# Pairwise bilinear products: later tiles of x loaded one by one from a second queue, with regular output slots

## The chip, the cores and the metric

The kernel runs on one core of a Trainium2 chip. The metric is the time of one execution on the device in microseconds (us), the median of several runs. A core has five engines that run their own instruction streams: TensorE (PE; its weight loads are PEld), VectorE (DVE), ScalarE (ACT), GpSimd (POOL) and SyncE (SP). Sixteen DMA engines move data between the chip's large memory (HBM) and the core's on-chip memory. A DMA transfer is started by an instruction on one engine's queue, and goes on beside everything else.

## The reference

For 4096 samples of 32 fields with 64 features each, every field is multiplied by a 64 x 64 matrix, and each of the 496 pairs of fields (i < j) gives one product by elements:

```python
vid = jnp.einsum('bfd,de->bfe', x, W)
idx_i, idx_j = jnp.triu_indices(F_, k=1)
return x[:, idx_i, :] * vid[:, idx_j, :]
```

Everything is float32. The input x has 33.6 MB, the output 520 MB.

## The kernel before

**Layout.** The host lays x out so that the 128 partitions are 2 halves of the batch x 64 features. A tile is 128 samples of each half; there are 16 tiles. One field of one tile is a *unit*: 128 float32 (512 B) in each partition. A tile of x has 32 units, 16,384 B per partition; its output has 496 units, one for each pair.

**On-chip memory.** One tensor, `mem`, holds 445 units for everything. Places for tiles of x and *slots* for output are cut out of it by hand: `XPLACE` says where each tile of x stands, and `SLOTS` lists for each output transfer its size in pairs and its place in `mem`. Places overlap in the course of time: an instruction that writes to a part of `mem` waits for the transfer that still reads that part, and for no other.

**Work on a tile.** TensorE multiplies the tile by W in 16 matmuls (L162) into `vid`, which has one place only[...]. VectorE then writes the products x[i] * vid[j] (L186) into the current slot, many pairs in one instruction, in the order that `by_block()` and `products()` give. When a slot is full, SyncE starts the transfer of it to the output (L189). An output transfer is cut in rows, one per partition: a slot of 127 pairs has rows of 127 x 512 = 65,024 B.

**Loads.** All transfers stand on SyncE's queue, in the order of the program. Tile 0 comes in two halves (L138). Then `GROUPS` says which tiles are loaded together: the first group, tiles 1 to 5, is loaded at the start. The second (tiles 6 to 10, in two transfers) is started at L192 to L194 when tile 4 is done, and the third (tiles 11 to 15, in two transfers) when tile 9 is done. A group is thus five tiles back to back. `SLOTS` has 80 entries whose sizes, 51 to 127 pairs, are chosen so that places for five tiles come free together before a group is loaded.

Of the kernel before, what the change touches and what calls it, by code (L numbers as in the profile page):

```python
# [16 lines left out]
UNITS = 445  # L17


GROUPS = [  # L20
    [[0], [1, 2], [3, 4], [5]],
    [[6, 7], [8, 9, 10]],
    [[12, 11], [15, 14, 13]],
]
XPLACE = [285, 317, 349, 381, 413, 0, 285, 317, 349, 381, 413, 128, 96, 64, 32, 0]


SLOTS = [
    (127, 32), (126, 159), (63, 32), (64, 95), (84, 159), (63, 32),
    (74, 243), (84, 159), (95, 32), (71, 243), (116, 127), (95, 32),  # L30
    (106, 243), (116, 127), (95, 32), (106, 243), (116, 127), (95, 32),
    (127, 243), (116, 127), (95, 32), (127, 243), (116, 127), (43, 370),
    (95, 32), (95, 127), (63, 222), (95, 32), (84, 127), (74, 211),
    (84, 32), (95, 116), (74, 211), (116, 0), (95, 116), (74, 211),
    (116, 0), (95, 116), (105, 211), (105, 0), (105, 105), (105, 211),
    (105, 0), (105, 105), (127, 211), (105, 0), (105, 105), (127, 211),
    (105, 0), (106, 105), (56, 211), (95, 267), (51, 362), (107, 160),
    (73, 267), (73, 340), (84, 160), (84, 244), (95, 340), (84, 160),
    (95, 244), (105, 340), (84, 160), (96, 244), (105, 340), (105, 128),
    (106, 233), (105, 339), (127, 96), (116, 223), (106, 339), (127, 96),  # L40
    (116, 223), (106, 339), (127, 64), (127, 191), (127, 318), (127, 32),
    (127, 159), (120, 286),
]


PAD = 24
# [2 lines left out]

STARTS = [0, *accumulate(n for n, _ in SLOTS)]  # L50


def by_block():


    def within(lo):
        yield "step", lo, 2, 1, 0
        for k in range(2):
            yield "step", lo, 4, 2, k
        for i in (lo, lo + 8):  # L60
            yield "row", i + 4, i, 4, 4
        yield "row", lo + 8, lo, 8, 8

    yield from within(0)
    yield "row", 16, 0, 16, 16
    yield from within(16)


def products(blocks, at=0):

    for kind, a, b, c, d in blocks:
        if kind == "row":
            rows, n, i0, di, j0, dj = c, d, b, 0, a, 1
        else:
            rows, n, i0, di, j0, dj = 16 // b, c, a, b, a + c + d, b
        r = k = 0
        while r < rows:
            room = STARTS[bisect_right(STARTS, at)] - at
            if k or room < n:
                m, w = 1, min(n - k, room)  # L80
            else:
                m, w = min(rows - r, room // n), n
            yield at, m, w, i0 + r * di + k, di, j0 + r * dj, dj
            at += m * w
            if k + w == n:
                r, k = r + m, 0
            else:
                k += w
# [10 lines left out]
@with_exitstack  # L99
def pairwise_bilinear_kernel(  # L100
    ctx: ExitStack,
    tc: tile.TileContext,
    x0: bass.AP,
    x: bass.AP,
    w: bass.AP,
    out: bass.AP,
):

    nc = tc.nc
    NT = sum(len(tiles) for group in GROUPS for tiles in group)
    F = x0.shape[1] - PAD0
    D = P // 2
    NP = F * (F - 1) // 2

    BANK = 512 // C


    ctx.enter_context(tc.manual_schedule(engines={mybir.EngineType.SP}))

    const = ctx.enter_context(tc.tile_pool(name="const", bufs=1))
    psum = ctx.enter_context(
        tc.tile_pool(name="ps", bufs=1, space=bass.MemoryType.PSUM)
    )
    vid = psum.tile([P, F, C], F32)

    mem = const.tile([P, UNITS, C], F32)  # L130


    w2 = const.tile([P, D], F32)


    for lo in (0, F // 2):
        place = XPLACE[0] + lo
        nc.sync.dma_start(out=mem[:, place : place + F // 2, :], in_=x0[:, lo : lo + F // 2, :])  # L138
        if lo == 0:
            nc.sync.dma_start(out=w2, in_=w)  # L140
    loaded = 1

    def load(tiles):
        nonlocal loaded
        n = len(tiles) * F
        place = XPLACE[tiles[0]]
        at = (loaded - 1) * F
        nc.sync.dma_start(out=mem[:, place : place + n, :], in_=x[:, at : at + n, :])
        loaded += len(tiles)

    groups = iter(GROUPS)
    for tiles in next(groups)[1:]:
        load(tiles)

    for t in range(NT):
        xt = mem[:, XPLACE[t] : XPLACE[t] + F, :]


        for b in range(0, F, BANK):
            for h in range(2):  # L160
                half = slice(h * D, (h + 1) * D)
                nc.tensor.matmul(  # L162
                    vid[half, b : b + BANK, :],
                    lhsT=w2[half, :],
                    rhs=xt[half, b : b + BANK, :],
                    start=True,
                    stop=True,
                )

        for at, m, w, i, di, j, dj in products(by_block(), t * NP):  # L170
            slot = bisect_right(STARTS, at) - 1
            n = m * w
            begin, end = STARTS[slot], STARTS[slot + 1]
            ot = mem[:, SLOTS[slot][1] : SLOTS[slot][1] + SLOTS[slot][0], :]
            o = ot[:, at - begin : at - begin + n, :]
            if m == 1:
                left = xt[:, i : i + w, :]
                right = vid[:, j : j + 1, :].to_broadcast([P, w, C])
            else:
                o = o.rearrange("p (m w) c -> p m w c", m=m)  # L180
                right = vid[:, j : j + (m - 1) * dj + 1 : dj, :].unsqueeze(2).to_broadcast([P, m, w, C])
                if di == 0:
                    left = xt[:, i : i + w, :].unsqueeze(1).to_broadcast([P, m, w, C])
                else:
                    left = xt.rearrange("p (m d) c -> p m d c", d=di)[:, i // di : i // di + m, i % di : i % di + w, :]
            nc.vector.tensor_tensor(o, left, right, ALU.mult)  # L186
            at += n
            if at == end:
                nc.sync.dma_start(out=out[:, begin:end, :], in_=ot)  # L189


        if t + 2 == loaded < NT:  # L192
            for tiles in next(groups):
                load(tiles)  # L194


_INS = ["r_x", "L0_rec_W"]
# [42 lines left out]
```

## Time and profile before

| | |
|---|---|
| Time, median of 3 runs | 1288.43 us (1288.34 to 1288.59) |
| Span in the profile | 1287.0 us |
| DMA, over the span | 553.79 MB, mean 430 GB/s |
| HBM | 33.59 MB read, 520.09 MB written |
| VectorE busy | 1087.8 us (85%), 407 instructions |
| TensorE busy | 225.4 us (18%), 512 matmuls |
| Output transfers | 80, of 3264 to 8128 KB |
| Loads of x after tile 0 | 7: 2048 KB x1, 4096 KB x4, 6144 KB x2 |

A group in the profile is a line, an engine, an operation and its tensors, with the number of instructions; then busy time and the mean duration of one; then the idle time of the engine just before these instructions, with what ended most of it. The slices give the busy share of each of 40 equal parts of the span in tenths (9 is 90% or more), and for DMA the rate too. q1 is the hardware queue of SyncE; q8 and q14 carry the chip's own fetching of instructions.

### The profile page before, as it was taken

The numbers are of one execution on the slowest core, as the hardware profiler recorded it, in microseconds if no ns is written. First come the engines' busy times: TensorE is split into PE (matmuls) and PEld (weight loads), VectorE is DVE, ScalarE is ACT, GpSimd is POOL, SyncE is SP. The second block draws the span as 40 slices with busy tenths as digits, with TensorE's granted clock in tenths as the row PEclk, the third lists the DMA queues.
The fourth block names the chain that finished last, engine by engine and source line by source line (L and its number), as shares of the span: only waits on it lengthen the run. The fifth ranks groups of instructions, "written<-read, shape, count | busy, mean of one in ns | idle before, by whom it ended". The sixth has DMA issues, their size and how long they took to land.

```text
span 1287.0 us, 1744 instructions
## 1 busy us (share of the span) xinstructions
PE 225.4 (18%) x512; PEld 41.6 (3%) x512; DVE 1087.8 (85%) x407; POOL 0.2 (0%) x4
## 2 busy tenths in 40 slices
PE   4031221312013013030313111103131121302000
PEld 1000000000000000000000000000000000000000
DVE  6799999998948399899999887369999998989960
POOL 0000000000000000000000000000000000000000
PEclk8555555556555555565655555555555555655555
DMA  9999999999999999999999999999999999999998
GB/s 411 432 427 431 442 432 430 437 434 433 435 422 419 425 430 433 438 432 438 428 439 436 428 440 421 427 430 435 434 438 428 439 435 439 434 430 437 430 434 368
DMA packets 12969, 553.79 MB, mean 430 GB/s; under 512 B 1568, under 2 KB 1568, under 8 KB 1568
## 3 DMA queue, kind: packets, MB, share of 16 engines
q1 hardware_dynamic: 12960, 553.69, 99.7%
q8 instruction: 4, 0.07, 0.0%
q14 instruction: 5, 0.04, 0.0%
HBM read 33.59 MB, written 520.09 MB: 430 GB/s over the span
## 4 chain that ended last, share of the span: by engine, by line
DMA 49%; DVE 44%; issue 3%; PE 0%; another core or an unknown queue 0%; DVEq 0%; SPq 0%
DMA out_dram<-mem 49%; DVE mem L186 44%; PE vid L162 0%; DMA w<-in_L_rec_W_dram 0%; DVEq L228 0%; DVEq L186 0%; SPq L138 0%
## 5 line engine op out<-in xcount | busy, mean ns | idle before, releaser
L186 DVE TENSOR_TENSOR mem<-mem,vid 128x1024 f32<-128x1024 f32 (+16 forms) x407 | 1087.8, 2748 | 155.0 <-DMA out_dram<-mem 143.3
L162 PE MATMUL vid<-mem,w 64*64 64x512 f32 x512 | 225.4, 1004 | 949.5 <-DVE mem L186 883.2
L162 PEld LDWEIGHTS vid<-mem,w 64*64 64x64 f32 x512 | 41.6, 198 | 1131.6 <-DVE mem L186 1033.3
L208 POOL MEMSET const-bfloat16-1.0<- 128x1 bf16 x1 | 0.1, 101 | 0.0
L208 POOL MEMSET const-uint8-127<- 128x1 uint8 x1 | 0.1, 101 | 0.0
L208 POOL MEMSET const-float32-0.0<- 128x1 f32 x1 | 0.1, 98 | 0.2 <-issue 0.2
L208 POOL MEMSET const-float32-1.0<- 128x1 f32 x1 | 0.1, 98 | 0.0
## 6 DMA issues: line engine op xcount, KB each, us to landing
out_dram<-mem SPq DMA_DIRECT2D x12, 8128.0 KB, 35.1
out_dram<-mem SPq DMA_DIRECT2D x13, 6720.0 KB, 32.9
out_dram<-mem SPq DMA_DIRECT2D x14, 6080.0 KB, 31.0
out_dram<-mem SPq DMA_DIRECT2D x9, 7424.0 KB, 31.6
out_dram<-mem SPq DMA_DIRECT2D x8, 5376.0 KB, 23.7
out_dram<-mem SPq DMA_DIRECT2D x6, 6784.0 KB, 34.6
out_dram<-mem SPq DMA_DIRECT2D x4, 4736.0 KB, 26.2
mem<-in_r_x_dram SPq DMA_DIRECT2D x4, 4096.0 KB, 21.8
```

Of the source, the lines that this page charges most:

```text
L162: nc.tensor.matmul(vid[half, b : b + BANK, :], lhsT=w2[half, :], rhs=xt[half, b : b + BANK, :], start=True, stop=True,)
L186: nc.vector.tensor_tensor(o, left, right, ALU.mult)
L208: nc = _bacc.Bacc("TRN2", target_bir_lowering=False, num_devices=1, dynamic_dma_scratch_size=1024)
```

## The change

Each later tile of x is loaded alone. Tiles 0 to 4 are loaded at the start, as before on SyncE's queue: tile 0 in two halves, tile 1 alone, tiles 2 to 4 together. The other 11 tiles are each loaded by one transfer on ScalarE's queue, which has nothing else to do. Two places (units 381 and 413) take turns for them: tile 5 is loaded when tile 0 is done, tile 6 when tile 1 is done, and from then on tile t + 2 when tile t is done.

With only two places for x, the rest of `mem` can be a plain ring of three output slots. They have 95 pairs at first, since tiles 2 to 4 still stand at units 285 to 380, grow to 105 and 116 as these are used up, and have 127 pairs from the sixth tile on. There are 68 output transfers. This takes the place of the list of 80 slots and of the groups, and lets the host keep the tiles in their own order.

```diff
-GROUPS = [
-    [[0], [1, 2], [3, 4], [5]],
-    [[6, 7], [8, 9, 10]],
-    [[12, 11], [15, 14, 13]],
-]
-XPLACE = [285, 317, 349, 381, 413, 0, 285, 317, 349, 381, 413, 128, 96, 64, 32, 0]
...
+HEAD = [[0], [1], [2, 3, 4]]
+PIECES = 1
+
+
+def place_of(t):
+
+    return (381, 413, 285, 317, 349)[t] if t < 5 else (381, 413)[(t - 5) % 2]
+
+
+def slots():
+
+    n = 0
+    left = 16 * 496
+    out = []
+    while left:
+        done = n // 496
+        room = (95, 95, 95, 105, 116)[done] if done < 5 else 127
+        k = len(out) % 3
+        size = min(room, left)
+        out.append((size, k * room))
+        n += size
+        left -= size
+    return out
...
-    ctx.enter_context(tc.manual_schedule(engines={mybir.EngineType.SP}))
+    ctx.enter_context(tc.manual_schedule(engines={mybir.EngineType.SP, mybir.EngineType.Activation}))
...
+    def load(queue, tile, lo, n):
+        place = place_of(tile) + lo
+        at = (tile - 1) * F + lo
+        queue.dma_start(out=mem[:, place : place + n, :], in_=x[:, at : at + n, :])
+
+    for tiles in HEAD[1:]:
+        load(nc.sync, tiles[0], 0, len(tiles) * F)
+
+    later = {}
+    for t in range(5, NT):
+        before = t - 5 if t < 7 else t - 2
+        later.setdefault(before, t)
...
-        if t + 2 == loaded < NT:
-            for tiles in next(groups):
-                load(tiles)
+        if t in later:
+            step = F // PIECES
+            for lo in range(0, F, step):
+                load(nc.scalar, later[t], lo, step)
```

## The prediction

> **What bounds the kernel now.** I read the page first (DMA slices, queue table, chain), then the waits of VectorE and of the issuing queue, then rates by stretch, then the records of single DMA packets (start, duration, bytes) that lie under those rates. The page:
>
> ```profile
> DMA  9999999999999999999999999999999999999998
> GB/s 411 432 427 431 442 432 430 437 434 433 435 422 419 425 430 433 438 432 438 428 439 436 428 440 421 427 430 435 434 438 428 439 435 439 434 430 437 430 434 368
> ...
> q1 hardware_dynamic: 12960, 553.69, 99.7%
> q8 instruction: 4, 0.07, 0.0%
> q14 instruction: 5, 0.04, 0.0%
> ...
> DMA 49%; DVE 44%; issue 3%; PE 0%; another core or an unknown queue 0%; DVEq 0%; SPq 0%
> ...
> L186 DVE TENSOR_TENSOR mem<-mem,vid 128x1024 f32<-128x1024 f32 (+16 forms) x407 | 1087.8, 2748 | 155.0 <-DMA out_dram<-mem 143.3
> ```
>
> The one queue in use, q1, is busy for 99.7% of 16 engines' span. The chain gives VectorE 44%, but that is no bound: VectorE idles 155.0 us, 143.3 of it for a slot still being stored. So the span is the bytes over the rate the DMA engines reach, plus a few us at the ends. Only three things can change it: bytes, rate, and holes in the feed. The waits say the feed has slack, since VectorE waits for stores:
>
> ```profile
> DVE mem L186 <- DMA out_dram<-mem: 143.3, 34, 27.6
> ...
> DVE mem L186 <- PE vid L162: 11.5, 1, 11.5
> ```
>
> Now the rate by stretch (busy times of PE, PEld, DVE, POOL; clock; DMA share; GB/s). The third and fifth stretch hold the two later groups of loads, five tiles each:
>
> ```profile
> 60.00:380.00 320.00, 63.86 (x136) 10.46 (x136) 291.38 (x121) 0.00 (x0) 0.54 1.00 433
> 390.00:425.00 35.00, 7.18 (x18) 1.89 (x16) 23.00 (x12) 0.00 (x0) 0.55 1.00 408
> 470.00:790.00 320.00, 64.90 (x144) 11.10 (x144) 299.75 (x115) 0.00 (x0) 0.53 1.00 434
> 795.00:830.00 35.00, 6.13 (x16) 1.77 (x16) 14.64 (x3) 0.00 (x0) 0.55 1.01 423
> 860.00:1250.00 390.00, 66.02 (x144) 11.46 (x144) 363.03 (x130) 0.00 (x0) 0.53 1.00 434
> ```
>
> Pure storing runs at 433 to 434 GB/s. A stretch with loads falls to 408 and 423 although the engines show as fully busy: 35 us x (433.5 - 408)/433.5 = 2.1 us lost in the first group, 0.8 us in the second. The packets say where. One packet is one partition's row, 8 rows per engine and transfer. Store rows take 2.400 us (65,024 B), 1.985 (53,760 B), 1.402 (37,888 B): a line of 36.8 ns per KB (of 1000 B) plus 8 ns. The excess over that line, summed over the run, is 3.97 us per engine. It is not spread evenly: nearly all of it sits where an engine changes from storing to loading or back: 0.92 and 0.93 us in the first group, 0.26 and 0.91 in the second, together 3.0; 0.2 to 0.7 in the head.
>
> **What the Trainium skill says.** "DMA: Bandwidth & Descriptors", section "Issuing engines are not separate DMA queues": transfers started by ScalarE run on the same 16 engines and interleave with SyncE's, so a second queue brings no bandwidth. No run here shows two busy queues yet. Same page, "Queues, rings and completion order": each engine takes turns between the queues that have work, one packet at a time, and a packet is typically 9 to 17 descriptors. The trace agrees on taking turns and differs on the grain: the nine packets of q8 and q14 that fell into the store stream each came between two rows of one transfer, so the turn is one row. Same page, "Where 436 GB/s comes from": a ceiling of 435.2 GB/s; the trace's 434 is at it, so nothing is to be won on rate. Same page, "Latency and other measured facts": memory access latency 0.2 us, 2 us under high load; a possible reason for the loss at a change of direction, which no run here proves.
>
> **The change, part by part.**
>
> Bytes: the same x and the same output. Transfers of output fall from 80 to 68, later loads become 11 of one tile instead of 4 of two or three tiles. Rows per engine: 12 x 8 fewer store rows at 8 ns save 0.8 us; 6 x 8 more load rows give back 0.4. So -0.4 us.
>
> VectorE: 379 instructions for 407. From the rows by form, 14,336 elements take 15,084 ns and 1,024 take 1,214 ns: 133 ns per pair and 147 ns per instruction, so 28 x 0.147 = 4 us less. Hidden, because VectorE waits for stores.
>
> Slots: three of 127 pairs. Filling one takes 127 x 0.133 + some 6 x 0.147 = 17.8 us, storing it 8 x 2.400 = 19.2 us. While one slot fills, one is stored and one is queued, so the feed has nearly a whole store of slack. In the head: the first slot of 95 pairs takes about 13.1 us after VectorE's start at 11.5 (before, 127 pairs were ready at 29.03), so it is ready at 24.7; five tiles of loads are done near 27 (before, six tiles ended near 32). No hole. Where slots grow (the 17th at pair 1520, the 22nd, the 26th) a new slot overlaps the place of the second-last one, so its last 20 or so pairs wait for that store and only one store covers them: some 3 us of filling plus 3.5 us of latencies against a 14.4 us store. VectorE stalls (6 to 11 us), the DMA engines hardly: I charge 1 us for all three.
>
> Waits of the loads: on ScalarE's queue each waits for the end of VectorE's tile t before loading t+2 into the same place. Behind it stand only further loads; ScalarE computes nothing. TensorE needs the tile one tile later, 75 us of storing; a load landing in 30 us is early. No cost.
>
> The old groups go: -3.0 us of changes of direction.
>
> The new loads: this is the open price. Each engine gets 11 x 8 = 88 load rows of 16,384 B that take turns with store rows of up to 65,024 B. The nearest rows are the four 16,384 B packets of q8 that fell alone into the stream: each took 0.88 to 0.96 us where 0.611 is normal for that size, and the store row after it 0.38 to 0.41 us more than normal, together 0.67 to 0.73, mean 0.70 us. The five 8,192 B packets of q14 cost 0.27 to 0.36 us, all on the store row after. If each load row costs what its like of 16,384 B cost, 88 x 0.70 = 61.6 us. From below: 0, if two busy queues hide it; from above: a change of direction on one queue cost up to 0.93 x 2 per visit, 88 x 1.86 = 164 us. I take 0.70: same size, same stream, row by row. The weak point is that those packets carried instructions, not x, and came alone.
>
> Sum: 1288.4 - 0.4 - 3.0 + 1 + 61.6 = 1347.6, rounded to 1348 us.
>
> **The rivals.**
> 1. Half price: only the store row after each load pays, as behind q14's packets: 88 x 0.35 = 30.8 us, so 1286.0 + 30.8 = 1317 us, where 1286.0 is the sum without the new loads. For it: five of nine packets did so. Against: their size is half a row of x.
> 2. A load goes through as one piece: an engine drains all 8 rows before turning back. Then a load costs one visit, 1.17 to 1.85 us as the two groups did: 11 x 1.5 = 16.6, so 1303 us. Against: nine of nine packets were served within a transfer.
> 3. The switches are hidden, because with rows waiting in both queues an engine reads ahead in the one while it writes for the other: 1288.4 - 0.4 - 3.0 + 1 = 1286 us, not slower than before. For it: the 8,192 B packets themselves took their normal 0.309 us. Against: within one queue, where reading ahead was possible too, each change still cost 0.3 to 0.9 us.
> 4. Worse: all engines read into a full stream of writes and a row pays near 1.2 us: 88 x 1.2 = 106, so 1392 us. Only the group changes, 0.9 us each, speak for it.
>
> **How the numbers follow.** Chances: forecast 0.46, half price 0.21, one piece 0.15, hidden 0.12, worse 0.06. The forecast's own spread of 0.5 to 0.95 us per row is 1330 to 1370. The range 1293 to 1370 takes in the forecast, half price and one piece and leaves out hidden and worse, 0.18. Faster by over 0.2% means under 1285.9, within means up to 1291.0: the hidden case at 1286 lies on that edge and splits 0.05 and 0.07, and one piece at its cheapest adds 0.01. So 0.05, 0.08, 0.87.
>
> **What would show it.** Right: a second hardware queue with 1,408 load rows; DMA share still near 100%; eleven dips of about 30 us each, in which a pair of rows (81,408 B) takes 0.611 + 2.400 + 0.70 = 3.71 us, so 16 engines move about 351 GB/s instead of 434; loads that need 25 to 30 us to land; VectorE waiting for stores by some 60 us more. Dips near 390 are half price, short dips of some 6 us with a load landing in about 8 us are one piece, no dips mean hidden. Wrong in another way: if the DMA share falls and the issuing queue waits for VectorE with nothing in flight, it was the slots and not the loads.

## The result and the profile after

The changed kernel takes 1299.66 us (median of 4 runs, 1299.04 to 1301.78) against 1288.51 us: 1.0088 times as long, interval 1.0074 to 1.0102. It is slower by 11 us; the forecast was slower by 60.

The page of the changed kernel, the lines that answer to those of before:

```profile
DMA  9999999999999999999999999999999999999996
GB/s 411 433 426 433 417 435 432 432 440 426 435 421 443 439 417 423 424 436 449 414 443 425 433 426 429 427 419 439 439 419 439 426 428 431 424 433 437 429 443 292
...
q1 hardware_dynamic: 10512, 530.62, 95.1%
q10 hardware_dynamic: 1584, 23.07, 4.2%
q8 instruction: 4, 0.07, 0.0%
q14 instruction: 5, 0.04, 0.0%
...
L187 DVE TENSOR_TENSOR mem<-mem,vid 128x1024 f32<-128x1024 f32 (+15 forms) x379 | 1087.3, 2941 | 170.3 <-DMA out_dram<-mem 157.9
...
out_dram<-mem SPq DMA_DIRECT2D x42, 8128.0 KB, 44.2
...
mem<-in_r_x_dram ACTq DMA_DIRECT2D x11, 2048.0 KB, 30.0
```

The second queue is there: q10 with 11 loads (1,408 rows and their completion packets). A load takes 30.0 us to land, so its rows do take turns with store rows. VectorE still waits for stores, and by 15 us more, so the ring of slots hardly starves the stores (a small exception follows). But the 351 GB/s dips of the forecast are missing: the lowest slice in the middle is 414. And the last slice is at 292 GB/s where before it was at 368. The last 32 us of both kernels, by stretch (columns as in the prediction), before and after:

```profile
1255.00:1287.00 32.00, 0.00 (x0) 0.00 (x0) 0.00 (x0) 0.00 (x0) 0.50 0.85 368
```

```profile
1266.00:1298.00 32.00, 0.00 (x0) 0.00 (x0) 0.00 (x0) 0.00 (x0) 0.50 0.67 290
```

Nothing computes there; only stores run. A DMA share of 0.67 means that some of the 16 engines have finished while others have a good way to go. The completion packets of the last store, one per engine, say how far: before, the first engine is done 3.6 us ahead of the last; after, 13.2 us.

So the sum of the difference, from the records of single packets, is this (us per engine; "lost rate" is the excess of all packets over the line of the prediction, "last behind mean" is how much later the slowest engine ends than the mean engine; gaps between packets have no row):

| | before | after | difference |
|---|---|---|---|
| rows and bytes on the line | 1279.7 | 1279.3 | -0.4 |
| lost rate | 4.0 | 9.6 | +5.6 |
| mean engine ends at | 1283.2 | 1289.0 | +5.8 |
| last behind mean | 2.4 | 7.7 | +5.3 |

Half of the 11 us is lost rate, half is that the engines run apart. The mean engine's end moves by 0.6 us more than the first two rows do. That is time without work: in the changed kernel the engines that are ahead stand idle at 267 and 365 us, where the slots grow, by 0.6 us on the mean; before, such gaps add up to 0.05. Here three loads in the changed kernel, by stretch:

```profile
617.00:643.00 26.00, 0.23 (x2) 0.00 (x0) 20.86 (x7) 0.00 (x0) 0.50 1.00 424
699.00:725.00 26.00, 0.20 (x2) 0.00 (x0) 21.17 (x7) 0.00 (x0) 0.50 1.00 423
780.00:806.00 26.00, 0.00 (x0) 0.00 (x0) 19.87 (x8) 0.00 (x0) 0.50 0.99 416
```

At 433 GB/s without a load, 424 is 0.5 us lost in 26 us, and 416 is 1.0. Row by row, most turns cost nothing: in the eleven stretches only 33 of 1,408 load rows and 339 of 1,681 store rows exceed the line by more than 0.06 us. So the loss falls on store rows, about one for every four load rows, and such a row loses 0.37 us on the mean. One load costs 0.4 to 1.1 us per engine on the mean. But from the sixth on the mean hides two groups: some ten engines lose 0.1 to 0.5 us in most loads, some six lose 1 to 2 us in most. (The records don't number the engines; they were told apart by packets that follow each other without a gap, so these counts are approximate.) The distance between the first and the last engine grows from 1.5 us (at 438 us) to 4.8 (685), 8.4 (811), 12.8 (1058) and 13.2.

### The profile page after: what moved, and what is told of

It reads as the page before. It is cut to its first block, busy times and chain, and to the rows that moved or that the text cites. A ratio compares the mean times of both kernels' runs of the same rounds, so it can differ in the third digit from the quotient of the medians.

```text
span 1298.2 us, 1741 instructions
## 1 busy us (share of the span) xinstructions
PE 216.5 (17%) x512; PEld 45.6 (4%) x512; DVE 1087.3 (84%) x379; POOL 0.2 (0%) x4
## 4 chain that ended last, share of the span: by engine, by line
DMA 56%; DVE 32%; issue 8%; PE 0%; DVEq 0%; SPq 0%
DMA out_dram<-mem 55%; DVE mem L187 32%; PE vid L163 0%; DMA w<-in_L_rec_W_dram 0%; DVEq L229 0%; DVEq L187 0%; SPq L140 0%
## 5 line engine op out<-in xcount | busy, mean ns | idle before, releaser
L187 DVE TENSOR_TENSOR mem<-mem,vid 128x1024 f32<-128x1024 f32 (+15 forms) x379 | 1087.3, 2941 | 170.3 <-DMA out_dram<-mem 157.9
L163 PE MATMUL vid<-mem,w 64*64 64x512 f32 x512 | 216.5, 981 | 969.5 <-DVE mem L187 716.9
L163 PEld LDWEIGHTS vid<-mem,w 64*64 64x64 f32 x512 | 45.6, 201 | 1139.1 <-DVE mem L187 847.0
```

Source lines behind the costliest of these rows:

```text
L163: nc.tensor.matmul(vid[half, b : b + BANK, :], lhsT=w2[half, :], rhs=xt[half, b : b + BANK, :], start=True, stop=True,)
```

## The experiments

**The loads or the slots.** The changed kernel, without its later loads:

```diff
-        if t in later:
+        if t in later and False:
```

> The changed kernel without its 11 later loads: from tile 5 on TensorE and VectorE work on whatever stands in the two places of x, so those outputs are not the reference's. Theory 'loads' (the whole loss comes from load rows among store rows: lost rate plus engines running apart): the bytes of the loads go (88 rows x 0.611 = 53.8 us) and so does all the loss, 1286 - 53.8 = 1232 us, with the 16 engines ending within about 3 us of each other. Theory 'slots' (the ring of three slots, its growth or the tail cost the 11 us): 1299.7 - 53.8 = 1246 us, and engines still end 13 us apart.

Measured: 1232.5 us, ratio 0.9566 (0.9551 to 0.958). With the 53.8 us of the loads' bytes that is 1286.3, where the forecast's sum without the new loads had 1286.0. The last 32 us:

```profile
1199.00:1231.00 32.00, 0.00 (x0) 0.00 (x0) 0.00 (x0) 0.00 (x0) 0.50 0.90 388
```

The engines end 2.2 us apart, and they have no gaps where the slots grow. So the slots, their growth and the tail cost nothing that shows by themselves; the loss comes with the loads: 1299.7 - 1286.3 = 13.4 us beyond their bytes, offset by 2.2 us that the rest saves.

**Taking turns or loading at all.** The same 11 loads on SyncE's queue, at the same point of the program:

```diff
-                load(nc.scalar, later[t], lo, step)
+                load(nc.sync, later[t], lo, step)
```

> The changed kernel with its 11 loads on SyncE's queue at the same point of the program: no rows of two queues take turns, each load is one visit of 8 rows per engine. Theory 'turns' (taking turns by rows loses the time and drives the engines apart): 11 visits at the price of the two groups before, 1.2 to 1.9 us each, so 1286 + 17 = 1303 us but with engines ending within 4 us; if a visit of only one tile is cheaper (0.5 us) 1291 us. Theory 'any load' (a load drives engines apart however it is queued): about 1300 us with engines 10 us or more apart.

Measured: 1293.78 us, ratio 1.0041 (1.0026 to 1.0056). Without turns the loads still cost 7.5 us beyond their bytes: 3.5 of lost rate over the run without loads (0.3 us a visit, cheaper than in the two groups before), and the engines end 7.0 us apart. Neither theory's numbers are met, but each holds in part: loads cost time and drive engines apart on one queue too, and taking turns with the stores costs 6 us more.

**A price per arrival or per row.** Each tile in four transfers of shorter rows:

```diff
-PIECES = 1
+PIECES = 4
```

> The changed kernel with each later tile in 4 transfers of 8 units, so 352 load rows of 4,096 B per engine in place of 88 of 16,384 B, same bytes, same 11 times. Theory 'visit' (an engine pays once when the load rows arrive, and later turns are hidden): within 4 us of 1300 us. Theory 'row' (every turn has its price, 0.09 us on the mean): 264 more rows x 0.093 = 25 us more of lost rate and some 16 us more of engines running apart, 1325 to 1340 us.

Measured: 1295.20 us, ratio 1.0052 (1.0037 to 1.0067). Neither theory: four times the rows cost less, not more. Lost rate over the run without loads is only 1.3 us, 0.004 us a row; against that stand 2.1 us for 264 more rows at 8 ns. The engines end 3.4 us apart, but not because short rows keep them together: at 1090 us they are 8.3 apart. Then a store waits on SyncE's queue, the engines are without work for some 3 us on the mean, and after that they are 3.8 apart:

```profile
1092.00:1100.00 8.00, 0.31 (x2) 0.32 (x4) 4.14 (x5) 0.00 (x0) 0.50 0.59 214
```

The profile puts this wait, 33.6 us long, down to a load that has not landed; why a store waits for it isn't shown. So the profiled run of this kernel has a hole that those with whole tiles and with halves (just below) don't have.

With two transfers a tile (PIECES = 2, rows of 8,192 B):

> The changed kernel with each later tile in 2 transfers of 16 units, 176 load rows of 8,192 B per engine. Theory 'row length': between four pieces (1295.2) and one (1299.7), with a lost rate between the two, 1296 to 1298 us. Theory 'visit' alone: 1300 us as with one piece.

Measured: 1296.31 us, ratio 1.0063 (1.0046 to 1.008), with 3.1 us of lost rate, 0.018 us a row, and engines 10.2 us apart. The time lies where the theory "row length" puts it.

**Fewer, longer rows.** Two tiles in one transfer:

```diff
-        room = (95, 95, 95, 105, 116)[done] if done < 5 else 127
+        room = 95 if done < 3 else 105
...
+            load(nc.scalar, later[t], 0, min(2, NT - later[t]) * F)
```

> The changed kernel with four places for x in place of two: later tiles come two by two in one transfer of 64 units (32,768 B rows; tile 15 alone), 6 transfers in place of 11, and slots stop growing at 105 pairs (78 stores). The loads cost 13.4 us beyond their bytes in the changed kernel. Theory 'visit' (a price per arrival): 6/11 of it, 7.3 us, so 1294 us. Theory 'row length' (longer load rows are hidden worse, 4,096 B rows being almost free): 48 rows of twice the length cost as much as 88, 1299 us or more.

Measured: 1293.50 us, ratio 1.0038 (1.0023 to 1.0053), the 1294 of the theory "visit": lost rate 3.7 us over the run without loads, engines 5.1 us apart. Half as many rows of twice the length cost about half, 0.077 us a row. Since this run has 6 arrivals for 11 and 48 rows for 88, it can't tell a price per arrival from one per row.

Each of these lost rates comes from one profiled run. A run further down with nearly the code of the changed kernel (the one with marks) lost 4.8 us over the run without loads where the changed kernel lost 6.6, so 0.055 us a row for 0.075. The step from 8,192 B (0.018) to 16,384 B is larger than that; the small differences among the others are not settled.

**The queue alone, in the kernel before.** Its two later groups on ScalarE's queue, as they are:

```diff
-        nc.sync.dma_start(out=mem[:, place : place + n, :], in_=x[:, at : at + n, :])
+        queue.dma_start(out=mem[:, place : place + n, :], in_=x[:, at : at + n, :])
...
-                load(tiles)
+                load(tiles, nc.scalar)
```

> The kernel before with its two later groups (4 transfers) on ScalarE's queue and nothing else changed: the queue alone. Theory 'visit': 2 arrivals at 0.7 us in place of the 3.0 us that the changes of direction cost on one queue, about 1287 us. Theory 'row': 32 rows at 0.09 us are 3 us, no difference on the mean, engines 2 us further apart, about 1290 us. Theory 'second queue is what costs': near 1300 us.

Measured: 1289.28 us (12 runs), ratio 1.0005 (0.9996 to 1.0014): no difference, and near the 1290 of the theory "row". A second queue as such doesn't cost the 11 us. Then the same with each tile of the two groups as a transfer of its own:

```diff
-                load(tiles, nc.scalar)
+                place = XPLACE[tiles[0]]
+                for k in range(len(tiles)):
+                    at = (loaded - 1) * F
+                    nc.scalar.dma_start(out=mem[:, place + k * F : place + (k + 1) * F, :], in_=x[:, at : at + F, :])
+                    loaded += 1
```

> The kernel before with its two later groups on ScalarE's queue, each tile of a group as a transfer of its own (10 transfers, 80 rows of 16,384 B per engine, in 2 arrivals). Theory 'visit': 2 arrivals of 0.75 us in place of 3.0 us of changes of direction, 1287 us, a little faster than before. Theory 'load rows of 16,384 B cost 0.09 us each and drive engines apart with each row': 80 rows cost as much as the 88 of the changed kernel, 1297 us.

Measured: 1300.05 us, ratio 1.0086 (1.0071 to 1.0102), the time of the changed kernel. The stretch of the first group and the last 32 us, with whole groups and with tiles one by one:

```profile
360.00:460.00 100.00, 12.57 (x30) 2.13 (x28) 57.57 (x24) 0.00 (x0) 0.52 1.00 422
...
1255.00:1287.00 32.00, 0.00 (x0) 0.00 (x0) 0.00 (x0) 0.00 (x0) 0.50 0.87 376
```

```profile
360.00:460.00 100.00, 12.96 (x30) 2.15 (x28) 57.55 (x24) 0.00 (x0) 0.52 1.00 417
...
1266.00:1298.00 32.00, 0.00 (x0) 0.00 (x0) 0.00 (x0) 0.00 (x0) 0.50 0.73 317
```

Slots, places and the queue are those of the run just before, and each group starts within 6 us of the same time. What differs is the rows, 80 of 16,384 B in place of 32 of 32,768 and 49,152 B, and with their number the time over which they take turns with stores: some 90 us a group, where the whole groups take less than 60. The rate falls and the tail empties as in the changed kernel (lost rate 9.2 us against 4.7, last engine 7.2 us behind the mean against 1.3). So neither the slots nor the second queue nor the spreading of the loads over the run is needed: the loss belongs to many load rows of 16,384 B between store rows. With the four pieces above, their number alone isn't it either. It also ends the theory "visit", since the rows came in two arrivals here and in no fewer just before.

**Why the price of a lone packet misled.** The same rows, but arriving one by one, tied to VectorE's progress:

```diff
+            while t - 1 in later and step < 8 and at >= t * NP + 50 * step:
+                g = (0, 2, 4, 6, 1, 3, 5, 7)[step]
...
+                nc.vector.tensor_tensor(tick[near, :], mem[near, p0, 0:1], ot[near, at - begin - 1, 0:1], ALU.mult)
+                rows = slice(g * 16, g * 16 + 16)
+                nc.scalar.dma_start(out=mem[rows, p0 : p0 + F, :], in_=x[rows, (new - 1) * F : new * F, :])
+                step += 1
```

> The changed kernel with each later tile in 8 transfers of 16 partitions, one row of 16,384 B for each engine, started one by one as VectorE has done another 50 pairs of the next tile (88 tiny VectorE instructions tie them to it). Bytes, row length and number of load rows per engine are those of the changed kernel; only that each row now comes alone. Theory 'a lone row pays, a row in a run of turns does not' (the price of 0.70 us that the forecast took from lone packets is right for lone packets): 88 x 0.70 = 62 us over 1286, 1348 us, at the least 88 x 0.35, 1317 us. Theory 'rows of x are cheap either way' (packets that fetch instructions are dearer than loads of x): 1300 us, as in the changed kernel.

Measured: 1308.70 us, ratio 1.017 (1.0149 to 1.0192). Both theories miss: lone rows are dearer than rows in a run, 0.22 us each in place of 0.075, but far from 0.70 on the mean. The mean hides a change in the course of the run. The stretches of tiles 5, 6, 7 and 9:

```profile
86.00:144.00 58.00, 4.99 (x12) 0.76 (x8) 49.79 (x24) 0.00 (x0) 0.50 1.01 395
168.00:233.00 65.00, 7.42 (x20) 1.34 (x16) 53.68 (x26) 0.00 (x0) 0.54 1.01 405
477.00:534.00 57.00, 8.02 (x10) 2.29 (x11) 51.61 (x20) 0.00 (x0) 0.51 1.00 409
633.00:696.00 63.00, 6.72 (x8) 1.88 (x9) 55.07 (x25) 0.00 (x0) 0.51 1.00 430
```

At 395 GB/s the eight rows of tile 5 cost 5.5 us, 0.69 each, just what the forecast took. At 430 those of tile 9 cost 0.5 us in all. The first and the last engine were 1 to 3 us apart during tile 5 and 1 to 4 during tile 7, and 5 to 6 during tile 9. Tile 6 doesn't fit this order: its rows cost some 4.5 us while the engines were 6 to 9 us apart. To see whether distance is a reason at all, all engines were made to start together again after tile 9:

```diff
+        if t == 9:
+            place = SLOTS[slot - 1][1]
+            nc.sync.dma_start(out=mem[:, place : place + 1, :], in_=x[:, :1, :])
```

> The kernel with lone rows once more, and after tile 9 the dummy load that makes all engines start again together. In the run with lone rows the eight rows of a tile cost 5.5, 4.7 and 3.3 us per engine for tiles 5, 6 and 7, while engines ran within 2 us of each other, and 0.4 to 1.5 us from tile 8 on, when they were 4 to 6 us apart. Theory 'in step' (a load row is dear when all engines turn to it together): after the drain the rows of tiles 11 and 12 cost 3 us or more per tile again, and fall as the engines come apart; total near 1313 us. Theory 'something of the early stretch' (the shorter store rows, the start): they cost 0.4 to 1.5 us per tile as before; total 1311 us or less.

Measured: 1316.91 us in a single run, beside 1288.24 before, more than either theory's total. The wait brings the engines from 5.4 us apart to 0.9. The eight rows of tile 11 cost 6.4 us, those of tile 12 2.9, and then 1.0 and 0.4; in the run without the wait tiles 11 and 12 cost 0.9 and 1.2. But tile 11 has to be taken apart: two of its rows came before the wait, and three ran during it, with no store beside them, and these make 3.7 us of the 6.4. The three rows after the wait cost 1.9 us, 0.64 each; without the wait the same three cost 0.15 each. The stretch right after the wait, and a later one:

```profile
830.00:864.00 34.00, 7.74 (x10) 2.15 (x11) 32.40 (x13) 0.00 (x0) 0.50 0.97 402
967.00:1032.00 65.00, 6.99 (x9) 1.98 (x10) 58.87 (x23) 0.00 (x0) 0.51 1.00 427
```

So lone load rows were dear again, late in the run, after the engines had been brought together. But the distance alone doesn't set the price. The expectation has the engines within 2 us of each other during tile 6, but the completion packets have them 6 to 9 apart; and tile 12 here still cost 2.9 us with the engines 4.5 to 6 us apart, a distance at which most other tiles cost 0.4 to 1.5. What else matters isn't shown.

**Why the engines run apart.** The same wait in the changed kernel, with its loads in runs of eight rows:

> The changed kernel with one row-sized dummy load after tile 9 that writes into the slot stored last, so that SyncE's queue waits until all stores have landed on all 16 engines and every engine starts again together. The five loads of tiles 11 to 15 follow. Theory 'lag feeds itself' (an engine that is behind when load rows come loses most): after the drain the engines run apart slowly, as after the first five loads (3 to 4 us at the end in place of 13), total between 1297 and 1300 us although the drain costs some 3 us of its own. Theory 'six slow engines' (the same engines lose at each load whatever their lag): the engines run apart again by 1.2 us a load, 6 to 8 us at the end, total 1302 to 1304 us.

Measured: 1301.62 us, ratio 1.0096 (1.0081 to 1.0112), single runs from 1298.55 to 1302.96. After the wait the distance grew from 0.2 to 5.1 us over four loads, since that of tile 11 still came before it; in the changed kernel the same four loads took it from 8.4 to 13.2, by 4.8. So the distance grew as fast from 0.2 us as from 8.4, and the theory that lag feeds itself isn't borne out. The other theory, the same slow engines each time, fits this growth: at its 1.2 us a load, four loads give 4.8. But the time lies between the two, and the growth doesn't say that they are the same engines. Two runs with marks on some engines were to show whether they are the same ones:

> The changed kernel with five tiny transfers after tile 4, over 12, 8, 4, 2 and 1 partitions, which fall on fewer than 16 engines and so mark engines in the trace. Time about 1300 us. Theory 'fixed engines': the engines that are last at the end belong to the same marked classes as in the next run. Theory 'chance or lag': the classes differ.

> The kernel before with its groups as 10 transfers of one tile on ScalarE's queue, and the same five marking transfers after tile 3. Time about 1300 us. Theory 'fixed engines': the engines last at the end are of the same classes as in the run before. Theory 'chance or lag': they differ.

Measured: 1299.95 and 1298.42 us, one run each. Where the marks could be told apart, the late engines belonged to several classes, and no class was late as a whole: of three engines that got no mark in the first run, two ended late and one with the first. Which engines lose, and why, stays open.

No version beat the kernel before.

## Why the prediction was wrong

- What bounds the kernel, and that no rate is to be won: right. The steady rate stayed at 433 GB/s.
- Bytes, VectorE, slots and waits: right in sum, in part by luck. The sum without the new loads was put at 1286.0, and the run without loads gives 1286.3. But the old groups were to give back 3.0 us, and the lost rate falls only from 4.0 to 3.0 there, while the last engine ends 0.8 us less behind the mean; and the 1 us charged for the slots' growth wasn't paid, since that run has no gap in the feed. The two misses nearly cancel.
- The turn at every row: right. Load and store rows alternate, and loads take 30.0 us to land.
- "If each load row costs what its like of 16,384 B cost, 88 x 0.70 = 61.6 us": this step failed. Measured, the new loads cost 13.4 us beyond their bytes, made of 6.6 us of lost rate (0.075 us a row), 6.1 us by which the slowest engine falls behind the mean more than without loads, and 0.7 left over, about the 0.6 us for which engines that are ahead stand idle where the slots grow. Two things were wrong in borrowing the price. The packets of q8 fetch instructions, and their price doesn't follow that of rows of x: in the runs without lone rows nearly all of them again cost 0.67 to 0.73 us with the store row behind them, and in the run with lone rows 0.72 to 0.86, where rows of x cost anything from 0.05 to 0.7. And a lone packet is not a row in a run: in steady alternation some three turns in four cost nothing. The prediction named this weak point, and then took the price undiminished for the likeliest.
- The rivals: none was right as a whole. The total came nearest to "one piece", 1303 us, but that is luck: this rival had the rows of a load go through together, and they do not. "Half price" has the place and the size of a single loss about right, since store rows pay and a paying row loses 0.37 us where it said 0.35, but it had one at every load row, and there is one for every four. "Hidden" is right for most turns and still not for the total.
- What no case contained: the loss falls unevenly on the 16 engines, nothing brings them together again after the slots have stopped growing, and the time is set by the last of them. That alone is +5.3 us of the difference of 11.
- The Trainium skill, "DMA: Bandwidth & Descriptors", section "Issuing engines are not separate DMA queues", says that transfers from several queues interleave on the same engines. The runs agree, and add that interleaving has a price when loads come in rows of 16,384 B between stores: 1.0086 times the time in the kernel before with nothing changed but its later loads.

## What to carry to other kernels

When a kernel is bound by its DMA engines, look at what loads among stores cost beyond their bytes. In this kernel the length and number of the load rows mattered most: 32 long rows per engine could stand on a second queue without a difference that shows, while 80 or 88 rows of 16,384 B there cost some 11 us, whether they came back to back or spread out, and 6 us of it went when the 88 stood on the queue of the stores. Look at the last slice of the DMA rate as well: a lower rate there with nothing else running can be the sign that the 16 engines have run apart, a loss that the busy share in the middle doesn't show; the completion packets of the last store confirm it. And a price read from a lone event isn't the price in a stream of such events: here it was nine times too high (0.70 us for 0.075).

## What the runs showed of the hardware

- Lost rate per load row among long store rows, by the row's length, loads in runs: 0.004 us at 4,096 B, 0.018 at 8,192, 0.075 at 16,384 (0.055 in the run with marks), 0.077 at 32,768, each from one profiled run. So for the same bytes rows of 4,096 and 8,192 B lost less rate here than rows of 16,384 B, but at 4,096 B the 2.1 us for more rows, at 8 ns each, weighed more than the 1.3 us of rate that was lost. Why 16,384 B costs so much more than 8,192 isn't shown.
- A lone row of 16,384 B among stores cost 0.69 us with the engines 1 to 3 us apart, and 0.64 after a wait that brought them within 1 us. From tile 8 on, with the engines 4 to 7 us apart, it cost 0.05 to 0.2 us; but in tile 6, at 6 to 9 us apart, it cost 0.6, so the distance isn't the whole of it.
- DMA engines with work always waiting kept their distance: between loads it stayed to within a few tenths of a us for over 100 us. Where it shrank by a microsecond or more at once, engines that were ahead had run out of work: from 2.9 to 1.9 us in the changed kernel at 267 us, from 8.3 to 3.8 with four pieces at 1092 us.
